# The last LayerNorm and GELU of a two-layer block, with y held on chip between its two passes

## Chip, cores and metric

The kernel runs on one core of a Trainium2 chip. The metric is the device time of one execution in microseconds. The time before the change is 19573.84 us, the median of three runs (19570.98 to 19581.24).

## The reference

The input x is 8 images of 384 channels by 64 x 64 positions, in float32. Two layers follow each other, each with a residual sum:

```python
# --- layer 0 (conv_preact) ---
x = x + _L0_conv_ref(_gn(x), ...)   # channel attention
# --- layer 1 (conv_preact) ---
x = x + _L1_conv_ref(_gn(x), ...)   # selective scan, four directions
```

The change concerns only the end of layer 1. There `y` is the merged output of the four scans, and is normalised over the 384 channels of each position (a token):

```python
yc = jnp.transpose(y, (0, 2, 3, 1))
mu = jnp.mean(yc, axis=-1, keepdims=True)
var = jnp.mean((yc - mu) ** 2, axis=-1, keepdims=True)
yc = (yc - mu) * jax.lax.rsqrt(var + LN_EPS) * ln_weight + ln_bias
y = jnp.transpose(yc, (0, 3, 1, 2)).astype(x.dtype)
return jax.nn.gelu(y, approximate=False)
```

The layer's input, called `x1` in the kernel, is added to this, and the sum is the output.

## The kernel before

The eight images are worked through one after the other. For each, `channel_attention` computes layer 0 and stores its result `x1` to a buffer in DRAM (`x1_d`, channels on the partitions), and `selective_scan` computes the scans of layer 1. It adds its four directions up in another DRAM buffer, `y_d` (4096 tokens by 384 channels): the scan makes pieces of 512 tokens by 128 channels, and each piece is loaded, added to and stored again (lines 986, 988 and 1002). The last pieces of the last direction touch all rows of `y_d`, so that no row of it is complete before the very last store.

What is left of an image is then to normalise its tokens, turn them back to channels on partitions, apply the GELU, add `x1`, and write the output. For the images 0 to 6 this lies inside the attention of the next image (`finishing`, lines 205 to 249 and further), mixed in with other work. For the last image there is no next one: `finish` does it alone, at the end of the program, with nothing beside it. It works in 16 parts of 256 tokens (`FT` is 256), each a block of 384 KB, in two passes:

- `token_norm` loads each part of y (line 1175, tiles `fy`, three buffers), takes `bn_stats` and `bn_aggr` of its two halves of 128 tokens on VectorE (1178, 1179), and after all 16 makes a root on ScalarE (1180), its reciprocal on VectorE (1181) and a shift (1182). The part is then dropped.
- `finish_part` loads the part of y a second time (1191) and the part of x1 (1192). ScalarE normalises the two halves as scale times y plus shift (1194), TensorE transposes six blocks of 128 x 128 into PSUM (1201), ScalarE applies the GELU with the channels' own weight and bias (1202), VectorE adds x1 (1206), and the sum is stored (1207). Its three tiles (`fr`: y, sum, x1) have four buffers each.

All transfers are issued from SP (SyncE), in one queue in order; an issue that has to wait holds up those behind it. Each transfer signals on one of eight semaphores in turn, and an issue waits for the last transfer that used its semaphore. The order of the instructions in `finish` is set by the framework's scheduler, since nothing there is pinned; it mixes the first loads of the second pass in between those of the first, up to the four buffers.

Elsewhere in the program the two operations that the new version uses already occur: `bn_stats` and `bn_aggr` pinned one after the other (lines 627 and 628, for the earlier images), `tensor_scalar` with a subtraction and a multiplication on VectorE (line 780, 128x512), and a tensor_add of 128x768 on GpSimd (line 249).

Of the kernel before, what the change touches and what calls it, by code (L numbers as in the profile page):

```python
# [9 lines left out]
F32 = mybir.dt.float32  # L10
AF = mybir.ActivationFunctionType
ALU = mybir.AluOpType
AX = mybir.AxisListType
PSUM = bass.MemoryType.PSUM

P = 128
C = 384
NJ = C // P
H = W = 64
L = H * W  # L20
CH = 512
NCH = L // CH
NT = L // P
# [22 lines left out]
FT = 256  # L46
# [49 lines left out]
def tile_channel_attention_then_selective_scan(ctx: ExitStack, tc: tile.TileContext, a: dict):  # L96
    nc = tc.nc
    x_d, out_d = a["x"], a["out"]
    B = x_d.shape[0]
# [5 lines left out]
    ident = const.tile([P, P], F32, name="ident")  # L105
# [5 lines left out]
    eps = const.tile([P, 1], F32, name="eps")  # L111
# [5 lines left out]
    small = {}  # L117
    for name in ("dt_bias", "Ds", "ln_w", "ln_b", "temp"):
        t = const.tile(list(a[name].shape), F32, name=name)
# [1044 lines left out]
                x_next = x_next, near["r"]  # L1164
        return y_d, x_next

    def token_norm(b, keep, work, y_d):

        mv = keep.tile([P, NT, 2], F32, name=f"fmv{b}")
        scale = keep.tile([P, NT], F32, name=f"fsc{b}")  # L1170
        shift = keep.tile([P, NT], F32, name=f"fsh{b}")
        n = FT // P
        for i in range(L // FT):
            y = work.tile([P, n, C], F32, tag="ft", bufs=3, name=f"fy{b}_{i}")
            nc.sync.dma_start(y, y_d[bass.ts(i, FT), :].rearrange("(l p) c -> p l c", p=P))
            for t in range(n):
                stats = work.tile([P, nc.vector.BN_STATS_DIM], F32, tag="fst", name=f"fst{b}_{i}_{t}")
                nc.vector.bn_stats(stats, y[:, t, :])
                nc.vector.bn_aggr(mv[:, n * i + t, :], stats)
        nc.scalar.activation(scale, mv[:, :, 1], AF.Sqrt, bias=eps)  # L1180
        nc.vector.reciprocal(scale, scale)
        nc.vector.scalar_tensor_tensor(shift, mv[:, :, 0], -1.0, scale, ALU.mult, ALU.mult)
        return scale, shift

    def finish_part(b, x1_d, y_d, i, scale, shift, room, psum, tag):

        n = FT // P
        cs = bass.ts(i, FT)
        y = room[0].rearrange("p (l c) -> p l c", c=C)
        o, xr = (t.rearrange("p (j l) -> p j l", l=FT) for t in room[1:])  # L1190
        nc.sync.dma_start(y, y_d[cs, :].rearrange("(l p) c -> p l c", p=P))
        nc.sync.dma_start(xr, x1_d[:, :, cs].rearrange("j p l -> p j l"))
        for t in range(n):
            nc.scalar.activation(
                y[:, t, :], y[:, t, :], AF.Identity,
                bias=shift[:, n * i + t : n * i + t + 1], scale=scale[:, n * i + t : n * i + t + 1],
            )
        for j in range(NJ):
            pz = psum.tile([P, CH], F32, tag=tag, name=f"pz{b}_{i}_{j}")
            for t in range(n):  # L1200
                nc.tensor.transpose(pz[:, bass.ts(t, P)], y[:, t, bass.ts(j, P)], ident)
            nc.scalar.activation(
                o[:, j, :], pz[:, :FT], AF.Gelu,
                bias=small["ln_b"][:, j : j + 1], scale=small["ln_w"][:, j : j + 1],
            )
        nc.vector.tensor_add(o, o, xr)
        nc.sync.dma_start(out_d[b, :, :, cs].rearrange("j p l -> p j l"), o)

    def finish(b, x1_d, y_d):
        with ExitStack() as st:  # L1210
            wp = st.enter_context(tc.tile_pool(name=f"fw{b}", bufs=1))
            work = st.enter_context(tc.tile_pool(name=f"f{b}", bufs=2))
            ps = st.enter_context(tc.tile_pool(name=f"fp{b}", bufs=4, space=PSUM))
            scale, shift = token_norm(B, wp, work, y_d)
            for i in range(L // FT):
                room = [
                    work.tile([P, FT * NJ], F32, tag=f"r{n}", bufs=4, name=f"fr{b}_{i}_{n}")
                    for n in range(3)
                ]
                finish_part(b, x1_d, y_d, i, scale, shift, room, ps, "pz")  # L1220

    x, st0 = load_x(0), x_stats(0)
    for j in range(NJ):
# [8 lines left out]
    for b in range(B):  # L1232
        x1, x1_d, stats1 = channel_attention(b, *x, before)
        y_d, x = selective_scan(b, x1, stats1)
        before = (b, x1_d, y_d)
    finish(*before)


# [47 lines left out]
```

## Time and profile before

| what | value |
|---|---|
| median of three runs | 19573.84 us |
| the profiled execution's own time | 19593.03 us |
| its span, first to last instruction | 19591.2 us |
| first reload of y in `finish` (SP issues it) | 19496.13 us |
| first statistics | 19499.56 us |
| root on ScalarE | 19528.14 us |
| first normalised part done on ScalarE (start) | 19529.31 us |
| last add of x1 | 19586.87 us |
| granted TensorE clock, mean | 0.954 |

Times in the lower rows are counted from the start of the span. The chain of waits names, for each stretch of time, what the program was waiting for in the end; the windows show how busy each engine was in a stretch; the DMA view counts what the 16 DMA engines moved and which share of their time the packets took. In groups of instructions, the first pair of numbers is the busy time in all (us) and the mean of one (ns), and the second part is the idle time of the engine just before them and what ended it. The engines are PE (TensorE), DVE (VectorE), ACT (ScalarE), POOL (GpSimd) and SP (SyncE); SPq is SP's issuing of transfers.

### The profile page before, as it was taken

To read this page: it belongs to the slowest core of one execution; us is meant where nothing else is said; L and a number is where in the kernel's file an instruction comes from. 1 tells how busy PE (TensorE), PEld (TensorE's weight loads), DVE (VectorE), ACT (ScalarE), POOL (GpSimd) and SP (SyncE) were. 2 spreads that over 40 slices of the span, in tenths; PEclk is the share of its full clock that TensorE was granted. 3 is DMA by queue.
4 is the path that set the end of the run, shared out by engine and by line. 5 is a ranking of instruction groups with operands and counts; after the bars stand their busy time and mean duration, and the time that the engine had idled before them with its cause. 6 is when DMAs were issued, how large, how long until landed. Compare 5 with 4: busy or idle time off the path is not lost.

```text
span 19591.2 us, 415258 instructions
## 1 busy us (share of the span) xinstructions
PE 17097.0 (87%) x166560; PEld 10219.2 (52%) x166560; DVE 18453.4 (94%) x17510; ACT 17584.1 (90%) x30011; POOL 16874.4 (86%) x7486
## 2 busy tenths in 40 slices
PE   7888888888888888888888888888888888888887
PEld 4555545555455554555545555455554555545554
DVE  7999989999899998999989999899998999989998
ACT  6999979999799987999879998899988999889998
POOL 4999959999599985999859998599985999869997
PEclk9999999999999999999999999999999999999998
DMA  1232322223222232232322323223232223322223
GB/s 47 84 97 97 112 89 83 94 97 111 91 86 94 95 109 89 87 97 96 109 85 87 97 97 108 85 87 97 97 108 92 83 95 97 106 93 88 94 93 124
DMA packets 1214410, 1849.25 MB, mean 94 GB/s; under 512 B 154209, under 2 KB 1018721, under 8 KB 1075265
## 3 DMA queue, kind: packets, MB, share of 16 engines
q1 hardware_dynamic: 1211616, 1822.57, 28.7%
q8 instruction: 1314, 21.53, 0.5%
q14 instruction: 616, 5.04, 0.1%
q10 hardware_dynamic: 864, 0.12, 0.0%
HBM read 1503.58 MB, written 318.77 MB: 93 GB/s over the span
## 4 chain that ended last, share of the span: by engine, by line
ACT 27%; PE 23%; DVE 15%; issue 4%; POOL 3%; DMA 1%; SPq 0%; DVEq 0%; ACTq 0%; POOLq 0%
ACT da L898 12%; ACT hc L949 10%; PE pt L943 10%; DVE h L922 10%; PE py L960 5%; PE px L810 3%; DVE ac L451 3%; POOL db L910 2%; ACT dt L872 1%; PE pp L599 1%; PE pd L864 1%; PE py L966 1%; ACT pr L413 1%; ACT L872 1%; ACT L898 1%
## 5 line engine op out<-in xcount | busy, mean ns | idle before, releaser
L910 POOL TENSOR_TENSOR db<-w,B 128x2048 f32<-128x2048 f32 x3072 | 14053.0, 4578 | 618.8 <-DVE h L922 514.7
L922 DVE TENSOR_TENSOR_SCAN h<-da,ca,db 128x512 f32<-128x512 f32 x10752 | 12786.6, 1263 | 305.3 <-ACT da L898 287.0
L898 ACT ACTIVATE da<-dt,neg_a 128x512 f32<-128x512 f32 x12288 | 8741.8, 713 | 157.6 <-DVE h L922 153.4
L943 PE MATMUL pt<-ident,h 128*128 128x128 f32 x49152 | 8127.0, 294 | 858.4 <-DVE h L922 505.8
L949 ACT COPY hc<-pt 128x512 f32<-128x512 f32 x12288 | 7393.0, 604 | 704.7 <-PE pt L943 641.1
L943 PEld LDWEIGHTS pt<-ident,h 128*128 128x128 f32 x49152 | 5452.3, 146 | 3314.2 <-issue 1912.0
L960 PE MATMUL py<-hc,cp 128*32 128x128 f32 x98304 | 5070.4, 290 | 893.4 <-ACT hc L949 726.0
L960 PEld LDWEIGHTS py<-hc,cp 128*32 128x32 f32 x98304 | 2050.1, 110 | 3164.5 <-ACT hc L949 1607.1
L922 DVE TENSOR_TENSOR_SCAN h<-da,db 128x512 f32<-128x512 f32 x1536 | 1748.2, 1206 | 115.8 <-ACT da L898 73.5
L420 POOL TENSOR_TENSOR pr<-pr,pr 128x1008 f32<-128x1008 f32 x288 | 673.3, 2338 | 1201.1 <-ACT pr L413 1184.0
L810 PE MATMUL px<-x,wx 128*44 128x128 f32 x6144 | 1219.8, 343 | 36.9 <-DVE cp L849 21.3
L881 POOL TENSOR_TENSOR w<-x,dt 128x512 f32<-128x512 f32 x744 | 1062.4, 1428 | 33.4 <-ACT dt L872 31.9
L810 PEld LDWEIGHTS px<-x,wx 128*44 128x44 f32 x6144 | 687.4, 128 | 367.0 <-issue 190.0
L864 PE MATMUL pd<-xd,wdt 128*128 128x512 f32 x1536 | 731.8, 613 | 157.0 <-DVE h L922 151.2
L426 POOL TENSOR_TENSOR pr<-pr,pr 128x1008 f32<-128x1008 f32 x288 | 574.8, 1996 | 277.2 <-ACT pr L413 193.8
L849 DVE TENSOR_TENSOR cp<-quad,pct 128x512 f32<-128x512 f32 x1024 | 628.2, 674 | 10.9 <-PE pct L838 10.9
L599 PE MATMUL pp<-v,mT 128*128 128x512 f32 x1152 | 539.1, 618 | 92.5 <-DVE v L456 91.4
L872 ACT ACT_TABLE_LOAD x256 | 328.4, 1283 | 229.1 <-PE pd L864 228.1
L936 POOL COPY ca<-h 128x4 f32<-128x4 f32 x2688 | 531.6, 198 | 0.0
L864 PEld LDWEIGHTS pd<-xd,wdt 128*128 128x128 f32 x1536 | 272.3, 190 | 465.4 <-issue 239.2
L872 ACT ACTIVATE dt<-pd,dt_bias 128x512 f32<-128x512 f32 x768 | 475.0, 686 | 8.2 <-PE pd L864 4.4
L1002 DVE TENSOR_TENSOR ys<-ys,py 128x512 f32<-128x512 f32 x576 | 383.9, 667 | 34.6 <-PE py L960 34.6
(334 smaller groups left out, 11500.5 us busy)
## 6 DMA issues: line engine op xcount, KB each, us to landing
B<-bcd SPq DMA_DIRECT2D x1024, 1024.0 KB, 4.8
yd<-ys SPq DMA_DIRECT2D x384, 256.0 KB, 3.4
ys<-yd SPq DMA_DIRECT2D x768, 128.0 KB, 2.9
yd<-ys SPq DMA_DIRECT2D x768, 128.0 KB, 4.3
x<-in_x SPq DMA_DIRECT2D x48, 1024.0 KB, 7.2
x1d<-x SPq DMA_DIRECT2D x192, 256.0 KB, 2.8
ys<-yd SPq DMA_DIRECT2D x192, 256.0 KB, 3.0
fy<-yd SPq DMA_DIRECT2D x128, 384.0 KB, 3.8
```

Source lines behind the costliest of these rows:

```text
L420: pin(nc.gpsimd.tensor_add(q[:, :, 1:], q[:, :, 1:], left[:, :, : W - 1]))
L599: pin(nc.tensor.matmul(pps[m, c], lhsT=fold_of[0][:, j, bass.ts(m, P)], rhs=vs["v"][:, j, bass.ts(c, CH)], start=j == 0, stop=j == NJ - 1,))
L810: pin(nc.tensor.matmul(split(pxs[s][:XR, :])[:, part, :], lhsT=wx[:, j, k, :], rhs=view(x1[j], k, c)[:, part, :], start=i == 0, stop=i == ...
L864: pin(nc.tensor.matmul(pd, lhsT=wdt[:, k, bass.ts(j, P)], rhs=xds[s], start=True, stop=True))
L872: pin(nc.scalar.activation(dts[s, j], pd, AF.Softplus, bias=small["dt_bias"][:, j, k : k + 1]))
L881: pin(eng.tensor_mul(split(ws[s, j]), view(x1[j], k, c), split(dts[s, j])))
L898: pin(nc.scalar.activation(t, dts[s, j], AF.Exp, scale=neg_a[:, j, steps[s][0], n : n + 1]))
L910: pin(eng.tensor_mul(t, w.broadcast_to([P, NV, CH]), bts[s, g]))
L922: pin(nc.vector.tensor_tensor_scan(h, da, db, 0.0 if start else carries[s - 1][:, j, n : n + 1], ALU.mult, ALU.add,))
L943: pin(nc.tensor.transpose(t[:, f, :], hs[u][:, bass.ts(q, HP), :].rearrange("p l v -> p (l v)"), ident))
L949: pin(nc.scalar.copy(t, pts.pop((u, lb))))
L960: pin(nc.tensor.matmul(py[f * HP : (f + 1) * HP, lb, :], lhsT=cps[s, g][:, q, :], rhs=hc[:, f, :], start=g == lb == 0, stop=g == NG - 1 an ...
```

## The change

`token_norm` and `finish_part` are gone; `finish` has all of it. Each of the 16 parts of y has a tile of its own (`ys`), and so has each part of x1 (`xs`), 16 tiles of 3 KB a partition for either. All y loads are issued first, then all x1 loads; y is loaded once. Statistics and aggregation alternate on VectorE. The normalisation is a `tensor_scalar` (subtract the mean, multiply by the scale) on VectorE, in place, so the shift is not needed. The six transposes of a part go into two PSUM tiles instead of three. The GELU writes its result into the y tile of the part. The add of x1 stands three parts behind the rest in program order; it writes into the x1 tile, and parts 1, 4, 7, 10 and 13 are added on GpSimd, the other 11 on VectorE. Every compute instruction is pinned to program order; the stores stand behind all loads in SP's queue.

```diff
-    def token_norm(b, keep, work, y_d):
...
-        for i in range(L // FT):
-            y = work.tile([P, n, C], F32, tag="ft", bufs=3, name=f"fy{b}_{i}")
-            nc.sync.dma_start(y, y_d[bass.ts(i, FT), :].rearrange("(l p) c -> p l c", p=P))
...
-    def finish_part(b, x1_d, y_d, i, scale, shift, room, psum, tag):
...
-        for t in range(n):
-            nc.scalar.activation(
-                y[:, t, :], y[:, t, :], AF.Identity,
-                bias=shift[:, n * i + t : n * i + t + 1], scale=scale[:, n * i + t : n * i + t + 1],
-            )
...
     def finish(b, x1_d, y_d):
+
+        pin = tc.keep_in_program_order
+        n, parts = FT // P, range(L // FT)
         with ExitStack() as st:
...
+            ys = [wp.tile([P, n, C], F32, name=f"fy{i}") for i in parts]
+            xs = [wp.tile([P, NJ, FT], F32, name=f"fx{i}") for i in parts]
+            for i in parts:
+                nc.sync.dma_start(ys[i], y_d[bass.ts(i, FT), :].rearrange("(l p) c -> p l c", p=P))
+            for i in parts:
+                nc.sync.dma_start(xs[i], x1_d[:, :, bass.ts(i, FT)].rearrange("j p l -> p j l"))
+            for i in parts:
+                for t in range(n):
+                    m = n * i + t
+                    pin(nc.vector.bn_stats(stats[:, m, :], ys[i][:, t, :]))
+                    pin(nc.vector.bn_aggr(mv[:, m, :], stats[:, m, :]))
+            pin(nc.scalar.activation(scale, mv[:, :, 1], AF.Sqrt, bias=eps))
+            pin(nc.vector.reciprocal(scale, scale))
+            for i in range(len(parts) + 3):
+                if i < len(parts):
+                    for t in range(n):
+                        m, v = n * i + t, ys[i][:, t, :]
+                        pin(nc.vector.tensor_scalar(
+                            v, v, mv[:, m, 0:1], scale[:, m : m + 1], ALU.subtract, ALU.mult
+                        ))
...
+                if i > 2:
+                    k = i - 3
+                    o = ys[k].rearrange("p l c -> p (l c)").rearrange("p (j l) -> p j l", l=FT)
+                    add = (nc.gpsimd if k % 3 == 1 else nc.vector).tensor_add
+                    pin(add(xs[k], xs[k], o))
+                    nc.sync.dma_start(
+                        out_d[b, :, :, bass.ts(k, FT)].rearrange("j p l -> p j l"), xs[k]
+                    )
```

More of the change, by code (lines that the diff above doesn't have):

```diff
@@ L1165, in selective_scan @@
         return y_d, x_next
-    def token_norm(b, keep, work, y_d):
[L1169 to L1172, printed above, removed]
-        for i in range(L // FT):
-            y = work.tile([P, n, C], F32, tag="ft", bufs=3, name=f"fy{b}_{i}")
-            nc.sync.dma_start(y, y_d[bass.ts(i, FT), :].rearrange("(l p) c -> p l c", p=P))
-            for t in range(n):
[L1177 to L1183, printed above, removed]
@@ L1185, in finish_part @@
-    def finish_part(b, x1_d, y_d, i, scale, shift, room, psum, tag):
[L1187 to L1194, printed above, removed]
-                y[:, t, :], y[:, t, :], AF.Identity,
-                bias=shift[:, n * i + t : n * i + t + 1], scale=scale[:, n * i + t : n * i + t + 1],
-            )
[L1198 to L1207, printed above, removed]
@@ L1209, in finish @@
     def finish(b, x1_d, y_d):
+        pin = tc.keep_in_program_order
+        n, parts = FT // P, range(L // FT)
         with ExitStack() as st:
[L1211 to L1220, printed above, removed]
+            wp = st.enter_context(tc.tile_pool(name=f"fw{b}", bufs=1, reuse_waits="tile"))
+            ps = st.enter_context(tc.tile_pool(name=f"fp{b}", bufs=4, space=PSUM, reuse_waits="tile"))
+            mv = wp.tile([P, NT, 2], F32, name="fmv")
+            stats = wp.tile([P, NT, nc.vector.BN_STATS_DIM], F32, name="fst")
+            scale = wp.tile([P, NT], F32, name="fsc")
+            ys = [wp.tile([P, n, C], F32, name=f"fy{i}") for i in parts]
[18 more added lines that the diff above has]
+                        ))
+                    pz = [ps.tile([P, CH], F32, tag=f"z{h}", name=f"fz{i}_{h}") for h in range(2)]
+                    for j in range(NJ):
+                        for t in range(n):
+                            pin(nc.tensor.transpose(
+                                pz[j // 2][:, bass.ts((j % 2) * n + t, P)], ys[i][:, t, bass.ts(j, P)], ident
+                            ))
+                    o = ys[i].rearrange("p l c -> p (l c)").rearrange("p (j l) -> p j l", l=FT)
+                    for j in range(NJ):
+                        pin(nc.scalar.activation(
+                            o[:, j, :], pz[j // 2][:, (j % 2) * FT : (j % 2 + 1) * FT], AF.Gelu,
+                            bias=small["ln_b"][:, j : j + 1], scale=small["ln_w"][:, j : j + 1],
+                        ))
+                if i > 2:
[6 more added lines that the diff above has]
+                    )
```

## Prediction

> **What bounds the kernel now.** The change touches only the last stage of the last image, so I read the span of the page (19591.2 us), then the chain of waits from 19,450 us on, the busy time by windows of the same stretch, the DMA view of three windows, the groups of instructions by shape, and SP's waits. Chain of waits (start, length, what):
>
> ```profile
> 19493.57 2.47 DMA yd<-ys
> 19496.13 3.26 DMA fy<-yd
> ...
> 19520.91 5.86 DMA fy<-yd
> 19526.87 1.02 DVE fst L1178 x2
> ...
> 19586.87 0.96 DVE fr L1206
> ```
>
> The scan's last store of y is followed by its first reload at 19496.13. From there to the end are 95.1 us, 0.49% of the span: 32 us of statistics, ended by the last fy load, then 63 us of normalising and writing. A transfer is what each step of the first pass waits for. Busy time by windows (microseconds; PE, PEld, DVE, ACT, POOL, clock, DMA share, GB/s):
>
> ```profile
> 19504.00:19512.00 8.00, 0.00 (x0) 0.00 (x0) 5.92 (x20) 0.00 (x0) 0.00 (x0) 0.50 0.97 315
> ...
> 19528.00:19536.00 8.00, 4.19 (x14) 2.45 (x14) 1.61 (x4) 6.98 (x12) 0.00 (x0) 0.50 0.18 57
> ...
> 19568.00:19576.00 8.00, 3.08 (x12) 2.09 (x12) 2.38 (x3) 4.92 (x10) 0.00 (x0) 0.50 0.97 317
> ```
>
> In both passes the DMA engines are nearly full at some 316 GB/s while no compute engine reaches 75% there. At the seam, 19528 to 19536, they stand idle: the four rooms of the second pass are full, SP's next load waits for a room, and ACT works nearly alone (it is full for one window more, 8.00 of 8 us to 19544). SP's waits have that stop as the longest of line 1191 (total, times, longest):
>
> ```profile
> SPq L1191 <- PE pz L1201: 12.0, 8, 8.9
> ```
>
> The DMA view's queue line (packets, MB, share of 16 engines) for 19500:19528, 19536:19584 and 19496:19592:
>
> ```profile
> q1 hardware_dynamic: 6382, 8.50, 93.7%
> ...
> q1 hardware_dynamic: 13238, 14.41, 94.9%
> ...
> q1 hardware_dynamic: 21504, 25.17, 81.8%
> ```
>
> The tail's own bound is therefore the volume of its transfers plus the idle time of the DMA engines: 0.818 x 96 = 78.5 us busy, and 95.1 - 78.5 = 16.6 us idle.
>
> **What the Trainium skill says.** "DMA: Bandwidth & Descriptors", section "Issuing engines are not separate DMA queues": all hardware queues run on the same 16 engines. So nothing but fewer bytes or fewer gaps helps; the trace agrees (share 0.97 with one queue). Its section "Queues, rings and completion order" says that an engine takes the descriptors of one ring in order: x1 loads stand behind the y loads issued before them, and stores behind both. That is consistent with fy15's 5.86 us (transfers ahead of it), but not proved by it. "SBUF — State Buffer", section "Who interferes with whom": VectorE in its two-port mode, or with two SBUF inputs, and GpSimd exclude each other for a whole instruction. The stage of before has no GpSimd work, so no row there shows it. "VectorE: DVE Perf Modes", section "The perf-mode tier table", puts float32 tensor_scalar at twice the rate of tensor_tensor; the trace: twelve of 128x512 in 5.56 us, 463 ns each, against 693 ns for a tensor_tensor of that size at line 881.
>
> **The change part by part.** Durations are from these rows (mean ns in the fifth place) and from the timeline:
>
> ```profile
> L1201 PE MATMUL pz<-ident,fr 128*128 128x128 f32 x96 | 28.2, 437 | 65.4 <-ACT fr L1194 64.2 <-ACT fr L1202 1.1
> L1202 ACT ACTIVATE fr<-pz,ln_b,ln_w 128x256 f32<-128x256 f32 x48 | 23.6, 560 | 6.0 <-PE pz L1201 6.0
> L1194 ACT ACTIVATE fr<-fr,fsh,fsc 128x384 f32<-128x384 f32 x32 | 20.8, 702 | 7.8 <-DMA fr<-yd 7.0 <-DVE fsh L1182 0.9
> L1178 DVE BATCH_NORM_STATS2 fst<-fy 128x6 f32<-128x384 f32 x32 | 16.3, 551 | 15.6 <-DMA fy<-yd 15.5
> L1206 DVE TENSOR_TENSOR fr<-fr,fr 128x768 f32<-128x768 f32 x16 | 15.3, 958 | 43.4 <-ACT fr L1202 43.4
> ```
>
> *Second load of y, removed.* Transfers of the tail go from 64 to 48, all of 384 KB; bytes from 25.17 to 18.87 MB. Each transfer adds 16 packets under 512 B (1,024 for 64). Without those, and solving the first two windows for two packet sizes (1,536 B for y; 1,024 B for x1 and out): window one has 6,037 data packets, so 4,527 of y and 1,510 others, 419.8 us of engine time; window two 2,828 and 9,830, 728.8 us. That gives 75.2 and 52.5 ns, so 256 x 75.2 / 16 = 1.20 us for a y transfer and 384 x 52.5 / 16 = 1.26 us for the others (check, third window: 8,192 x 75.2 + 12,288 x 52.5 = 1,261 us, against 0.818 x 96 x 16 = 1,256). Removed: 16 x 1.20 = 19.2 us. Left: 16 x 1.20 + 32 x 1.26 = 59.6 us.
>
> *Loads of x1 into their own rooms, all loads ahead of all stores.* On SP the order is now 16 y, 16 x1, 16 out. From the ninth on, an issue waits for the landing of the one eight before it, so eight are in flight: 8 x 1.2 = 10 us of work against issues of 0.36 to 0.6 us. Before, SP waited for VectorE's statistics (15.6 us at L1175), PE (12.0 us at L1191) and the adds (35.0 us at L1207), with loads behind the waiting issue. The x1 loads no longer wait for rooms and fill the seam. What stays idle: 1.4 us at the start (the first window 19496 to 19504 has share 0.81 of 8 us), 1.5 us from the last byte to the end (an estimate: SP waits 1.9 us for the last out, and the span ends 1.0 us later), and 2% in between, 1.2 us. Bounds of that: 0 and 7% (the shares above), 0 to 4.5 us. New tail 59.6 + 4.1 = 63.7 us.
>
> *Statistics.* bn_stats and bn_aggr now alternate. Line 627 and 628 do so in each earlier image: 0.66 us a pair, 1.32 a part. That is slightly longer than a y transfer, so pass one ends by VectorE: first landing 19499.4, plus 16 x 1.32 = 19520.5, then root and reciprocal (0.32 + 0.35 + gaps), 19521.5 against 19529.3 before. None of it is on the path, as the x1 transfers run on beside it. The shift (0.19 us) goes.
>
> *Normalisation on VectorE.* ACT loses 32 activations (20.8 us). VectorE gets 32 tensor_scalar of 128x384: between 0.23 us (three of 128x128 take 0.68) and 0.46 us, by line 0.385, so 0.77 us a part. With 11 of 16 adds at 0.96, 0.66 us, that makes 1.43 us a part. ACT keeps three Gelus at a pitch of 0.45: 1.36 us. PE keeps six transposes: 1.54 us for six in the timeline. The GELU table load (1.28 us) now stands straight after the root, beside VectorE and PE.
>
> *Five adds on GpSimd.* 128x768 took 1,818 ns at line 249. If it excludes VectorE: 3 x 1.43 = 4.3 us of three parts become 6.1, so 2.04 us a part; if not, 1.54 (PE). Hence the last add ends between 19521.5 + 4 + 16 x 1.54 = 19550 and 19521.5 + 4 + 16 x 2.04 = 19558. A store cannot move before the x1 loads are through, 19497.5 + 32 transfers (39.4 us) = 19537; then 16 x 1.26 = 20.2 us more, 19557. So the transfers end last, or, in the worst of the two, together with the adds (last add 19558, a store of 2.5 us, 1 us to the end: 19561.7). I take the transfers. Cover that is gone: an add waiting for x1 or for a Gelu holds up, in VectorE's order, the normalisation of the part four further on; the lag of three parts is 3 x 1.43 = 4.3 us, against 0.77 + 1.54 + 1.36 = 3.7 us that a part takes through three engines. That leaves little room, but 0.5 us a part lost there is still within the 2.04.
>
> Sum: the tail ends at 19496.1 + 63.7 = 19559.8, 31.4 us sooner. The profiled execution took 19593.03 us, 1.8 outside its span, and lies 19.2 above the median 19573.84; nothing of the tail explains that, so I take the saving from the median: 19542.5, 0.16%.
>
> **Rivals.** *The transfers run faster than their record* (0.15). Reads alone and then writes alone, with a queue never empty. For: single slices of the tail show 368 GB/s, and 19537 to 19541 a share of 1.01. Against: pass one is all reads and gave 324 at full share. At 368, 18.87 MB take 51.3 us, the tail 54.2, saving 41: 19533.
> *VectorE and GpSimd become the bound* (0.17). For: the exclusion above, the adds in order behind each other. At 2.04 to 2.4 us a part the end is 19561.7 to 19567.5: saving 24 to 29.5, 19547.
> *The rooms bring nothing early* (0.05). x1 stands behind y in one ring, and if eight in flight fill the engines to the 0.937 of pass one alone, 59.6 / 0.937 = 63.6, tail 66.5, saving 28.6: 19545.
> *Slower* (0.03): exclusion in full, so that each VectorE instruction of pass two waits out a GpSimd add and each add VectorE. Place: the loop of pass two; it decides only from (19588 - 19525.5) / 16 = 3.9 us a part, where before is reached, and 6.3 us for 0.2% more: 19613. Against: five GpSimd adds are 9.1 us in all.
>
> **How the numbers follow.** The forecast as worked out has 0.60; the two small rivals lie beside it, all three within 0.2% of before, which is 39.1 us and about what a measurement of this kernel can tell from no change. Half the spread of the three runs (5 us) can carry the 41 below that bound, and without any gaps the forecast's own saving (32.6) above it: of the 0.15 I count 0.10 as faster, of the 0.60 another 0.07. So faster 0.17, within 0.80, slower 0.03. Range: savings of 24 to 41 and 5 us on either side: 19528 to 19555, and above to 19560, since the base is three runs and the profiled execution lay 19 above them.
>
> **What would show it.** A share of the DMA engines over 0.95 from 19498 to the end; y, x1, out as three blocks of 19 to 20 us each; the last fst near 19520; SP's waits by DMA rather than by PE; ACT idle half of pass two. Wrong, if the DMA share falls under 0.9 after 19537 with adds at the end of the chain, or if the GB/s of a block is over 350.

## The result, and the profile after

The changed kernel takes 19539.85 us against 19575.14 us before (medians of 22 runs each, taken in turn). The ratio is 0.9984, with a 95% interval of 0.9977 to 0.9990: 0.16% less, about 35 us, below the 0.2% that was called the bound of no change, though the interval leaves out 1.

All of it lies in the tail, which is measured here from SP's first load of y in the last stage to the end of the span. Before, it went from 19496.13 to 19591.2 us: 95.1 us. In the changed kernel the first load is issued at 19480.55 and the span ends at 19540.5: 60.0 us. The tail is 35.1 us shorter (33.7 by a second profile of the changed kernel, below; of the kernel before there is one profile). The spans differ by 50.7 us, but 15.6 of these lie ahead of the tail, where both programs have the same instructions in the same order; that is the spread from run to run (the 22 runs before cover 38 us), and no part of the change. For this reason the experiments below are compared by their tails.

The windows of the changed kernel (columns as before: length, then PE, PEld, DVE, ACT, POOL, clock, DMA share, GB/s):

```profile
19484.00:19492.00 8.00, 0.00 (x0) 0.00 (x0) 7.44 (x23) 0.00 (x0) 0.00 (x0) 0.50 1.03 349
19492.00:19500.00 8.00, 0.00 (x0) 0.00 (x0) 7.57 (x25) 0.00 (x0) 0.00 (x0) 0.50 1.07 371
19500.00:19508.00 8.00, 1.28 (x5) 1.07 (x6) 7.30 (x23) 1.59 (x2) 0.00 (x0) 0.50 1.10 349
19508.00:19516.00 8.00, 6.21 (x39) 5.05 (x37) 7.83 (x13) 7.96 (x19) 2.86 (x2) 0.86 1.09 348
19516.00:19524.00 8.00, 4.63 (x21) 3.87 (x20) 8.00 (x12) 5.95 (x13) 4.11 (x2) 0.56 1.09 375
19524.00:19532.00 8.00, 6.13 (x32) 5.02 (x31) 8.00 (x14) 6.08 (x14) 2.67 (x2) 0.71 0.64 228
```

Two things are to be seen. From 19484 to 19524 the DMA engines are never all idle: the seam between the passes is gone, and they move 348 to 375 GB/s. The kernel before moved 304 GB/s over its first pass and 300 over its second (8.50 MB in 28 us and 14.41 MB in 48 us, by the queue lines of the prediction); the 316 named there stands for its better windows. The share is over 1, since packets overlap and each is counted with its whole time: the trace has up to 23 packets under way at once on 16 engines. After 19524 the share falls to 0.64, while VectorE is busy for the whole of the windows from 19516 to 19532. This says that VectorE, not the transfers, sets the end; the experiments test it.

The groups of the tail (busy, mean ns of one, idle before):

```profile
L1205 ACT ACTIVATE fy<-fz,ln_b,ln_w 128x256 f32<-128x256 f32 x48 | 22.4, 596 | 4.0 <-PE fz L1200 4.0
L1194 DVE TENSOR_SCALAR fy<-fy,fmv,fsc 128x384 f32<-128x384 f32 x32 | 19.2, 656 | 0.0
L1213 POOL TENSOR_TENSOR fx<-fx,fy 128x768 f32<-128x768 f32 x5 | 12.1, 2418 | 59.7 <-DMA fx<-x1d 48.4 <-ACT fy L1205 8.1 <-DMA out<-fx 3.2
L1213 DVE TENSOR_TENSOR fx<-fx,fy 128x768 f32<-128x768 f32 x11 | 11.6, 1065 | 0.4 <-ACT fy L1205 0.4
```

VectorE has almost no idle time in pass two, but its instructions are longer than their work: the 32 normalisations take 19.2 us, 0.60 each. The timeline shows where (start, length, instructions in a row):

```profile
19506.18 3.21 DVE L1194 TENSOR_SCALAR fy<-fy,fmv,fsc 128x384 f32<-128x384 f32 x8
...
19514.36 0.86 DVE L1194 TENSOR_SCALAR fy<-fy,fmv,fsc 128x384 f32<-128x384 f32 x2
...
19515.08 2.67 POOL L1213 TENSOR_TENSOR fx<-fx,fy 128x768 f32<-128x768 f32 x1 [2.11 <-ACT fy L1205]
...
19516.01 3.13 DVE L1194 TENSOR_SCALAR fy<-fy,fmv,fsc 128x384 f32<-128x384 f32 x4
...
19520.95 2.36 POOL L1213 TENSOR_TENSOR fx<-fx,fy 128x768 f32<-128x768 f32 x1 [3.21 <-DMA out<-fx]
...
19521.57 3.13 DVE L1194 TENSOR_SCALAR fy<-fy,fmv,fsc 128x384 f32<-128x384 f32 x4
...
19533.01 3.12 DVE L1213 TENSOR_TENSOR fx<-fx,fy 128x768 f32<-128x768 f32 x2 [0.22 <-ACT fy L1205]
```

Eight in a row take 3.21 us, 0.40 each. Where an add on GpSimd is running, four take 3.13 us instead of 1.60. The pattern repeats every 5.56 us, three parts: 1.85 us a part.

SP's waits (total, times, longest) have changed sides too. In the last stage before, SP waited for VectorE's statistics and adds with loads behind the waiting issue:

```profile
SPq L1207 <- DVE fr L1206: 35.0, 16, 3.5
SPq L1175 <- DVE fmv L1179: 15.6, 13, 1.4
```

Now the stores alone wait for compute, and no load stands behind them:

```profile
SPq L1214 <- DVE fy L1194: 7.6, 4, 2.2
SPq L1214 <- DVE fx L1213: 5.2, 6, 1.2
SPq L1214 <- POOL fx L1213: 4.8, 4, 1.2
```

### The profile page after: what moved, and what is told of

It reads as the page before. It is cut to its first block, busy times and chain, and to the rows that moved or that the text cites. A ratio compares the mean times of both kernels' runs of the same rounds, so it can differ in the third digit from the quotient of the medians.

```text
span 19540.5 us, 415194 instructions
## 1 busy us (share of the span) xinstructions
PE 17058.0 (87%) x166560; PEld 10193.3 (52%) x166560; DVE 18463.4 (94%) x17536; ACT 17563.2 (90%) x29979; POOL 16887.1 (86%) x7491
## 5 line engine op out<-in xcount | busy, mean ns | idle before, releaser
L881 POOL TENSOR_TENSOR w<-x,dt 128x512 f32<-128x512 f32 x744 | 1064.1, 1430 | 33.7 <-ACT dt L872 31.6
```

The costliest lines, as they stand in the source:

```text
L881: pin(eng.tensor_mul(split(ws[s, j]), view(x1[j], k, c), split(dts[s, j])))
```

## The experiments

The theory after the result (A): the loads run faster than reckoned because up to eight transfers are in flight, and pass two is set by VectorE, which GpSimd's adds hold up. The rivals: the loads are faster because a block of them is of one kind; the normalisations are slow for another reason; the transfers set the end after all; one part of the change alone brings the whole gain. Each tail in the table is that of one profile.

| kernel | tail, us |
|---|---|
| before | 95.1 |
| changed; the same once more | 60.0; 61.3 |
| changed, all adds on VectorE | 56.7 |
| changed, all adds on VectorE, statistics ahead of aggregation | 55.1 |
| transfers and statistics alone | 54.9 |
| changed, all adds on VectorE, a quarter of the normalisation on ScalarE, statistics ahead | 61.2 |
| changed, y loaded twice | 72.8 |
| changed, x1 in four rooms | 72.9 |
| changed, loads of y and x1 alternating | 73.6 |
| before, with y kept on chip only | 74.7 |
| changed, y loaded twice with three buffers | 78.7 |
| before, with eight buffers for the first pass | 87.5 |
| changed, normalisation on ScalarE | 91.3 |

**All adds on VectorE.**

```diff
-                    add = (nc.gpsimd if k % 3 == 1 else nc.vector).tensor_add
+                    add = nc.vector.tensor_add
```

> The changed kernel with all 16 adds of x1 on VectorE, none on GpSimd. Read on the tail: from SP's first load of y in the last stage to the end of the span, 60.0 us in the changed kernel. Theory A (VectorE and GpSimd exclude each other): the tensor_scalar instructions that took 0.78 us each beside a GpSimd add (four in 3.13 us) all take 0.39 to 0.40, VectorE does 32 x 0.39 + 16 x 0.95 = 27.7 us of work without gaps instead of 30 us, and the tail is 57.5 to 58.5 us, although VectorE has five adds more. Rival B (the tensor_scalar instructions are slowed by the stores or by ScalarE's and TensorE's traffic): they stay at 0.78 us, VectorE needs five adds more, and the tail grows by about 5 us to 65. Rival C (the transfers set the end): tail unchanged at 60.

Groups of this kernel's tail:

```profile
L1213 DVE TENSOR_TENSOR fx<-fx,fy 128x768 f32<-128x768 f32 x16 | 15.0, 958 | 0.2 <-ACT fy L1205 0.2
L1194 DVE TENSOR_SCALAR fy<-fy,fmv,fsc 128x384 f32<-128x384 f32 x32 | 13.6, 479 | 0.0
```

Its timeline, first normalisations and last adds:

```profile
19515.71 3.21 DVE L1194 TENSOR_SCALAR fy<-fy,fmv,fsc 128x384 f32<-128x384 f32 x8
...
19538.86 3.56 DVE L1213 TENSOR_TENSOR fx<-fx,fy 128x768 f32<-128x768 f32 x4
```

The tail is 56.7 us, 3.3 shorter than with five adds on GpSimd, though VectorE has five adds more. The 32 normalisations take 13.6 instead of 19.2 us, 0.43 each, no pair of them as slow as before. From the first normalisation to the last add VectorE needs 26.7 us (19515.71 to 19542.42) instead of 30.0 (19506.18 to 19536.13). So GpSimd's adds held VectorE up, and they cost more than they took over. Rivals B and C fall. The tail is a little under the expected 57.5 to 58.5 us.

**Transfers alone.** The edit leaves out the root and all of pass two but the stores:

```diff
-            pin(nc.scalar.activation(scale, mv[:, :, 1], AF.Sqrt, bias=eps))
-            pin(nc.vector.reciprocal(scale, scale))
...
+            for i in parts:
+                nc.sync.dma_start(out_d[b, :, :, bass.ts(i, FT)].rearrange("j p l -> p j l"), xs[i])
```

> The changed kernel without the second pass's arithmetic: root, normalisation, transposes, Gelu and add are left out, and x1 is stored as it was loaded; all 48 transfers and the statistics remain. It measures the floor of the transfers. Theory A (overlapping packets, 350 to 375 GB/s): 18.87 MB in 51 to 54 us and a tail of 54 to 57 us. The forecast's sum (59.6 us of packet times at a share of 1): tail 62 to 64 us, which the changed kernel with 60.0 already speaks against.

The GB/s over 40 slices of 1.35 us, from 19466 to 19520:

```profile
GB/s 327 376 291 361 372 391 378 374 372 374 372 374 365 353 347 348 349 348 348 350 347 347 348 349 347 349 378 383 384 387 383 384 387 382 388 383 385 379 92 0
q1 hardware_dynamic: 17119, 18.83, 102.9%
```

Three plateaus: y in packets of 1,536 B at about 373 GB/s, x1 in 1,024 B at 348, stores in 1,024 B at 384. The tail is 54.9 us, as A had it. The second line counts packets, MB and the share of 16 engines over the 54 us: the packets took 1.029 x 54 = 55.6 us in all. The changed kernel is 5.1 us above this floor (6.5 in its second profile); that is what the waiting for VectorE costs.

**A version between the two.** To bring VectorE below the floor, four parts of sixteen are normalised on ScalarE, all adds are on VectorE, and the two bn_stats of a part precede its two bn_aggr:

```diff
...
-                    pin(nc.vector.bn_stats(stats[:, m, :], ys[i][:, t, :]))
-                    pin(nc.vector.bn_aggr(mv[:, m, :], stats[:, m, :]))
+                    pin(nc.vector.bn_stats(stats[:, n * i + t, :], ys[i][:, t, :]))
+                for t in range(n):
+                    pin(nc.vector.bn_aggr(mv[:, n * i + t, :], stats[:, n * i + t, :]))
...
+                        if i % 4 == 3:
+                            pin(nc.scalar.activation(
+                                v, v, AF.Identity, bias=shift[:, m : m + 1], scale=scale[:, m : m + 1]
+                            ))
+                        else:
...
```

> The changed kernel with all adds on VectorE, the normalisation of every fourth part on ScalarE (four of sixteen), and each part's two bn_stats ahead of its two bn_aggr. Theory A: statistics 16 x 1.23 instead of 1.32 us, VectorE in pass two 24 x 0.39 + 16 x 0.95 = 24.6 us, ScalarE 48 x 0.46 + 8 x 0.6 = 26.9 us; last add some 27 to 28 us after the root, and the transfers nearly at their floor: tail 55 to 57.5 us. Rival (transfers or ScalarE's waits for TensorE already set the end): 59 to 61 us.

A miss: 61.2 us. The waits of this kernel:

```profile
PE fz L1207 <- ACT fy L1197: 9.8, 6, 2.8
DVE fx L1220 <- ACT fy L1212: 9.7, 10, 2.8
```

ScalarE's instructions are pinned to program order. The normalisation of such a part stands behind the Gelus of the part ahead, so TensorE waits for it, ScalarE's next Gelus wait for TensorE, and VectorE's adds wait for these: 9.7 us that were not there. The sum of busy times balanced; the order did not. The same without the move:

> The changed kernel with all adds on VectorE and each part's two bn_stats ahead of its two bn_aggr; nothing moved to ScalarE. Theory A (VectorE sets the end, and its work is statistics 16 x 1.13 to 1.32 us plus 27.7 us in pass two): with the shorter statistics the tail goes from 56.65 us (all adds on VectorE alone) to about 54.9 to 56, where the transfers' floor of 54.86 is reached. Rival (stores are what is left): 56.5 or more. In time, 4 to 5 us of 19,540 against the changed kernel is far below what runs can tell: ratio to before 0.9975 to 0.999.

The tail is 55.1 us, 0.2 above the floor, which is a tie. Statistics of two parts, and the last two windows with full transfers:

```profile
19487.71 0.99 DVE L1185 BATCH_NORM_STATS2 fst<-fy 128x6 f32<-128x384 f32 x2
...
19488.83 0.99 DVE L1185 BATCH_NORM_STATS2 fst<-fy 128x6 f32<-128x384 f32 x2
...
19515.09:19523.09 8.00, 5.31 (x30) 3.28 (x30) 8.00 (x15) 7.48 (x17) 0.00 (x0) 1.00 1.09 381
19523.09:19531.09 8.00, 2.13 (x12) 1.33 (x12) 5.63 (x9) 3.93 (x9) 0.00 (x0) 0.89 1.09 384
```

A part's statistics take 1.12 us instead of 1.32, and the stores now run at 381 to 384 GB/s. The kernel before already had its statistics in this order, two bn_stats ahead of two bn_aggr; the change gave it up. So the move of a quarter to ScalarE cost 6.1 us by itself. In time the ratio to before is 0.9981 (0.9973 to 0.9988). The changed kernel, run beside it, tells whether the two can be told apart by time:

> The changed kernel once more, beside the version with all adds on VectorE: the tail from the first load of y to the end is 59.5 to 60.5 us again, if it is a property of the program; the rest of the span may differ by 15 us, as it did between the two profiles on the page. Ratio to before 0.9975 to 0.999.

Its ratio is 0.9983 (0.9976 to 0.9990): the two overlap, and the better version shows only in its tail. The repeated tail, 61.3, missed its expectation: the first statistics waited 8.2 instead of 6.4 us for y. Tails of one kernel are thus known to within 1.4 us at best; the 3.3 us of the first experiment are above that, the 1.6 between 56.7 and 55.1 hardly.

**What the number of transfers in flight does.** First the kernel before, with eight buffers for the first pass:

```diff
-            y = work.tile([P, n, C], F32, tag="ft", bufs=3, name=f"fy{b}_{i}")
+            y = work.tile([P, n, C], F32, tag="ft", bufs=8, name=f"fy{b}_{i}")
```

> The kernel before with eight instead of three buffers for the first pass's loads of y, nothing else: eight transfers in flight instead of three or four, and reads only, as before. Theory A (the reads of the changed kernel run at 350 GB/s instead of 316 because more transfers are in flight): the first pass shows 345 to 355 GB/s at a DMA share over 1.03. Rival B (they run faster because the block is pure, without x1 loads in between and with one size of packet): in this kernel the first pass is then pure too, so the two are not told apart by the rate of y alone; but the packets' mean time, 75 ns by my sum for y, should fall if purity is the cause and stay or rise if overlap is. Tail by A: pass one ends by VectorE some 5 us sooner (16 x 1.25 us of statistics), but the second pass now begins with empty rooms behind the y loads in SP's queue: about 90 to 97 us, no clear gain.

Windows of the first pass:

```profile
19484.00:19494.00 10.00, 0.00 (x0) 0.00 (x0) 7.90 (x27) 0.00 (x0) 0.00 (x0) 0.50 1.00 354
...
19492.00:19502.00 10.00, 0.00 (x0) 0.00 (x0) 10.00 (x35) 0.00 (x0) 0.00 (x0) 0.50 1.07 371
```

354 to 371 GB/s, in a kernel that is otherwise the one of before; the share in the first window is 1.00, not over 1.03 as expected. The tail is 87.5 us, 7.6 shorter, better than the expected 90 to 97. As the expectation says, this run is deep and pure at once. The sign that it names for purity, a fall in the packets' mean time, did appear: the packets of 1,536 B took 69 ns each from 19484 to 19502, against 76 in the first pass of the kernel before (19502 to 19526). Two more runs take depth and purity apart. One issues the loads of y and x1 in turn (eight in flight, mixed); the other loads y twice with three buffers (few in flight, all of one kind):

```diff
             for i in parts:
                 nc.sync.dma_start(ys[i], y_d[bass.ts(i, FT), :].rearrange("(l p) c -> p l c", p=P))
-            for i in parts:
                 nc.sync.dma_start(xs[i], x1_d[:, :, bass.ts(i, FT)].rearrange("j p l -> p j l"))
```

> The changed kernel with the loads of y and x1 issued in turn, y0, x0, y1, x1 and so on: eight in flight, but two sizes of packet and two sources mixed. Theory A (the rate follows the number of transfers in flight): 345 to 375 GB/s in the block of loads. Rival B (it follows the purity of the block): 300 to 325 GB/s. Tail in both: y15 lands only with the 31st load, some 36 us after the first by A, so the second pass starts 12 us later than in the changed kernel: 70 to 74 us by A, 74 to 78 by B.

```diff
+            once = [wp.tile([P, n, C], F32, name=f"fo{i}") for i in range(3)]
+            for i in parts:
+                y = once[i % 3]
+                nc.sync.dma_start(y, y_d[bass.ts(i, FT), :].rearrange("(l p) c -> p l c", p=P))
...
```

> The kernel that loads y twice, with three instead of eight buffers for the statistics: all transfers of pass one are of y and of one size, but only three or four are in flight, since a load waits for VectorE. Theory A (number in flight): 290 to 325 GB/s in pass one, against 371 to 375 with eight buffers. Rival B (purity): 345 to 375 GB/s. Another reading of A, that the rate is no property of the engines but of SP waiting for VectorE, would show in the share: below 0.98 with gaps, not near 1.

Windows, two of the mixed kernel and then four of the one with three buffers:

```profile
19485.98:19493.98 8.00, 0.00 (x0) 0.00 (x0) 4.70 (x14) 0.00 (x0) 0.00 (x0) 0.50 1.08 360
19493.98:19501.98 8.00, 0.00 (x0) 0.00 (x0) 5.45 (x16) 0.00 (x0) 0.00 (x0) 0.50 1.08 360
```

```profile
19476.25:19484.25 8.00, 0.00 (x0) 0.00 (x0) 5.94 (x19) 0.00 (x0) 0.00 (x0) 0.50 0.85 263
19484.25:19492.25 8.00, 0.00 (x0) 0.00 (x0) 5.24 (x16) 0.00 (x0) 0.00 (x0) 0.50 0.85 283
19492.25:19500.25 8.00, 0.00 (x0) 0.00 (x0) 6.47 (x19) 0.00 (x0) 0.00 (x0) 0.50 0.90 292
19500.25:19508.25 8.00, 2.12 (x9) 1.92 (x10) 6.00 (x18) 2.40 (x4) 0.00 (x0) 0.50 1.05 369
```

Mixed and deep: 360 GB/s, which is what 373 for y and 348 for x1 give half and half. Pure and shallow: 263 to 292, below the 290 to 325 expected but for one window. In the last window the same kernel has its remaining loads of y queued without a wait for VectorE, and they run at 369. Purity falls: what decides is how far ahead the loads are queued. The packets' mean time follows this too, and not purity: 71 ns for 1,536 B in the mixed kernel, 75 in the shallow windows of the other.

By what means a short queue is slower is settled only in part. A share of 0.85 to 0.90 is the sign that the expectation named for gaps while SP waits for VectorE (16.1 us in its waits); the packets also overlap less and take longer. In the trace there is no moment in these windows at which nothing moves, but for a third of the time fewer than 14 packets are under way, and the record does not say which engines then stand idle. These runs do not separate a rate of the engines from the gaps.

Neither kernel's tail says anything about rate: the mixed one has 73.6 us because its pass two starts 39.7 us after the first load, 14.1 later than in the changed kernel, which is why y goes first.

**What each part of the change is worth.** Undone in the changed kernel, one at a time: y loaded a second time (through eight buffers for the statistics),

> The changed kernel with y loaded a second time: the statistics read it from eight buffers in turn, then sixteen loads bring it into its sixteen tiles, then x1 follows. All else as changed. Theory A (the bytes of the second load count in full, as the queue is never empty): 16 transfers of 384 KB more, at 350 GB/s 1.12 us each, so the last x1 lands 18 us later; the stores, which stand behind, begin later and then have their data ready, so they run at full rate: tail 73 to 78 us. Rival (the second load is hidden behind the statistics and the compute of pass two): tail 60 to 64 us.

72.8 us, so 12.9 more, just under the expected 73. The 16 loads cost 17.6 us (the first load of x1 is issued 30.4 us after the first of y instead of 12.8), but 5 come back: with the stores later, their data is ready, and they run at 383 to 386 GB/s. x1 in four rooms:

```diff
-            xs = [wp.tile([P, NJ, FT], F32, name=f"fx{i}") for i in parts]
+            xs = []
...
+            def load_x1(i):
+                xs.append(wp.tile([P, NJ, FT], F32, tag="fx", bufs=4, name=f"fx{i}"))
+                nc.sync.dma_start(xs[i], x1_d[:, :, bass.ts(i, FT)].rearrange("j p l -> p j l"))
+
+            for i in range(4):
+                load_x1(i)
...
+                    if k + 4 < len(parts):
+                        load_x1(k + 4)
```

> The changed kernel with x1 in four rooms in turn instead of sixteen, so that a load of x1 waits for the store that emptied its room; y stays on chip, normalisation on VectorE. Theory A (the early x1 loads fill the time of statistics and the seam): the DMA engines fall idle from the fourth x1 load until the first stores, and each later part waits for a store to land and a load to land, in turns of three: 3 stores and 3 loads in 7.5 us plus two latencies of 2.5 us, so about 4 us a part for twelve parts, and a tail of 75 to 85 us. Rival (keeping y alone brings the gain, the rooms bring nothing early): tail 60 to 64 us.

The busy share of the DMA engines in tenths, in 40 slices of 1.8 us from 19478:

```profile
DMA  8989999999995000042899969899899969999791
```

72.9 us, 12.9 more, a little under the expected 75. The zeros are the seam again: the four rooms are full, and nothing can move until the first stores. The normalisation on ScalarE (with a shift, which is computed as in the kernel before):

```diff
...
-                        pin(nc.vector.tensor_scalar(
-                            v, v, mv[:, m, 0:1], scale[:, m : m + 1], ALU.subtract, ALU.mult
-                        ))
+                        pin(nc.scalar.activation(
+                            v, v, AF.Identity, bias=shift[:, m : m + 1], scale=scale[:, m : m + 1]
+                        ))
```

> The changed kernel with the normalisation back on ScalarE (scale and shift, as before), all else as changed. Theory A (a compute engine sets the end): ScalarE does 32 x 0.60 + 48 x 0.46 = 41 us of work in order, with a wait for TensorE between a part's normalisation and its Gelu (some 0.6 us a part), so 16 x 3.2 = 51 us for the second pass and a tail of 75 to 82 us. Theory of the forecast (the transfers set the end, compute has room): ScalarE at 2.6 us a part gives 41 us, the last add 48 us after the start of pass two; tail 70 at least. Rival (normalisation can be hidden anywhere): 60 us.

91.3 us, more than the expected 75 to 82, for the reason that also spoilt the version between the two. Its timeline:

```profile
19506.36 1.30 ACT L1196 ACTIVATE fy<-fy,fsh,fsc 128x384 f32<-128x384 f32 x2
...
19508.72 1.48 ACT L1207 ACTIVATE fy<-fz,ln_b,ln_w 128x256 f32<-128x256 f32 x3 [1.05 <-PE fz L1202]
19510.08 1.30 ACT L1196 ACTIVATE fy<-fy,fsh,fsc 128x384 f32<-128x384 f32 x2
```

A part takes 3.72 us: two normalisations, 1.05 us of waiting for TensorE, three Gelus, and the next part cannot begin earlier. In the kernel before, the scheduler had put the next part's normalisation ahead of the Gelus for the first half of pass two. The 31.3 us that this run costs are therefore not the price of normalising on ScalarE alone: a good part is the price of this order, as the next run shows. It goes the other way round, the kernel before with y kept on chip and nothing else:

```diff
-            y = work.tile([P, n, C], F32, tag="ft", bufs=3, name=f"fy{b}_{i}")
+            y = keep.tile([P, n, C], F32, name=f"fy{b}_{i}")
+            ys.append(y)
...
-        nc.sync.dma_start(y, y_d[cs, :].rearrange("(l p) c -> p l c", p=P))
```

> The kernel before with one part of the change: y has sixteen tiles and is not loaded a second time. Normalisation stays on ScalarE, x1 in four rooms, stores and x1 loads mixed. Theory A (each part alone gives back what the others bring, as ScalarE's order of normalise, wait, Gelu and the four x1 rooms set the pace): pass one ends 5 us sooner by VectorE, pass two takes 16 x 2.65 to 3.3 us = 42 to 53 us; tail 72 to 82 us. Rival (bytes are all that matters): 48 transfers in 54 to 60 us, tail 60 to 64 us.

74.7 us, 20.4 less than before, as A had it: of the 35 us it brings over a half. Not all of that is the second load: with sixteen tiles the first loads of y no longer wait for rooms either, and depth alone brought 7.6 us above. ScalarE has 44.4 us of work in it (23.6 of Gelu, 20.8 of normalisation) and waits 0.6 us for data in each of its two groups; it sets the end. Its stores show the pace, with the next part's normalisation ahead of the Gelus:

```profile
19518.16 0.38 SPq L1207 DMA_DIRECT2D out<-fr  x1
...
19520.80 0.38 SPq L1207 DMA_DIRECT2D out<-fr  x1
```

That is 2.64 us a part against 3.72 in the pinned order. By an estimate from these two, 16 x 1.08 = 17 of the 31.3 us are the order and some 14 the engine; the changed kernel with ScalarE's work in the better order was not run. So no part brings the whole; undone one by one they cost 12.9, 12.9 and 31.3 us, together more than the 35, as each limits what the others can bring. The pinning and the two PSUM tiles were not undone alone.

## Why the prediction was right, and where its steps were not

**Verdict and size.** Forecast: no change beyond 0.2%, a saving of 31.4 us, 0.16%. Measured: 35.1 us in the tail, about 35 in the medians, 0.16%. Right, but with little room: at the floor of the transfers, 54.9 us, the saving would have been 40 us, 0.21%. That the size came within 4 us was in part luck. Two steps were off in opposite directions: the transfers were put 8.8 us too long, and the end was put on them, while the kernel stands 5.1 us above their floor.

**The transfers: the sum's term was too large.** "Left: 16 x 1.20 + 32 x 1.26 = 59.6 us", with 4.1 us around it, gave 63.7. The floor measured with the transfers alone is 54.9. About half of the 8.8 us is in the packets: they took 55.6 us, not 59.6. The two packet times were read rightly from the kernel before, but they do not stay what they were: in the trace of the transfers alone a packet of 1,536 B takes 71 ns on average (75.2 reckoned), one of 1,024 B takes 51 as a load and 46 as a store (52.5 reckoned for both). The other half is that 4.1 us of idle time were added where packets overlap instead: shares of 1.03 to 1.10 are sustained for 40 us, so the tail is 0.7 us shorter than its packets put end to end. The window of before with a share of 1.01 had shown it, and I took it for an exception. The rival "the transfers run faster than their record" had the floor nearly right (54.2), and its objection, that pass one is all reads and was slow all the same, left out that its queue was short. For the same reason "nothing but fewer bytes or fewer gaps helps" was too narrow, as far as the share of 0.97 was its support: eight buffers in the kernel before raised 304 to 354 and 371 GB/s with the same bytes.

**Which engine ends last: wrong.** "I take the transfers." It was VectorE: with all adds on it and the statistics reordered the tail falls to the floor of the transfers, 55.1 us. The rival was named with the right mechanism and, at 2.04 us a part, a price above the measured 1.85; a GpSimd add of 2.4 us takes 1.5 us from VectorE rather than the 1.8 that I reckoned. With the transfers faster than I thought, that was enough to leave them behind. Both signs that the prediction named against itself appeared: a DMA share under 0.9 with the adds at the end, and blocks over 350 GB/s. The Trainium skill ("SBUF — State Buffer", "Who interferes with whom") says that such instructions of VectorE and GpSimd exclude each other; the trace agrees in kind, with 1.60 against 3.13 us for four normalisations, and GpSimd's add is longer too, 2,418 ns against 1,810 in the kernel where ScalarE normalises.

**Pass one: right.** VectorE was to end it; from the first load to the first normalisation 25.4 us were forecast, 25.6 measured, with 0.66 us a pair of bn_stats and bn_aggr as in the earlier images.

**The seam and the x1 loads: right in kind.** The idle time that vanishes was put at 16.6 - 4.1 = 12.5 us, and the zeros of the four-room kernel show where it lies. That taking the early loads away costs 12.9 us is close by chance in part: that kernel also makes every later load of x1 wait for a store.

**The second load of y:** 19.2 us forecast for its transfers. In the queue they took 17.6. The tail changes by 20.4 when y alone is kept, with longer queues as a part of that, and by 12.9 when the load alone is put back, since the stores then lose their wait for VectorE.

**The normalisation:** I priced it as work that fits beside the transfers, which it does where no add runs on GpSimd (0.40 us each, 0.385 forecast). The factor of two between tensor_scalar and tensor_tensor that the prediction cites is 1.5 in the figures beside it, 463 against 693 ns; the measured ones were used. I gave no price for leaving it on ScalarE; undone in the pinned order, it costs the most of the three, 31.3 us.

## What to carry to other kernels

A transfer-bound stage has a floor that can be measured by leaving the arithmetic out; a share of 1 in the profile is not that floor if packets can overlap. Queue loads well ahead of what they wait for: here that alone raised the rate. Before work is moved to an idle engine, look at whom that engine shuts out and what stands behind the moved instruction in its queue: both moves here (adds to GpSimd, a quarter of the normalisation to ScalarE) balanced the sums and made the stage longer. In a kernel this long, compare the stage that was changed, since the rest of the span moves by more than the gain.

## What was not expected of the hardware

With up to eight transfers of 384 KB in flight the DMA engines held 348 to 384 GB/s once the first few microseconds were over. Where SP's waits left three or four in flight, they moved 263 to 292 GB/s in windows of the three-buffer kernel and 300 to 304 over the passes of the kernel before (a single window there reached 339). Stores of 1,024 B packets ran at 384 GB/s, loads of the same packets at 348. Whether more than eight in flight would give more was not tried. Why loads and stores of one size differ stays open, as do why packets get shorter in a long queue and the 1.4 us between two tails of the same program.
